# Deformable convolution: a table of pixel pairs, indices in two groups, four gathers issued at once

## Chip, cores and metric

The kernel runs on one core of a Trainium2 chip. The metric is the device time of one execution in microseconds (us); lower is better. Names of engines: PE is TensorE, DVE is VectorE, ACT is ScalarE, POOL is GpSimd, SP is SyncE, which here only issues DMAs.

## What is computed

The network has four residual layers over four images of 56 x 56 pixels with 128 channels, float32: window attention (L0), a selective-scan block (L1), a deformable convolution (L2), window attention again (L3). Each layer gets the group-normalized input and its result is added to the input. The change is in the third layer, whose reference is, cut:

```python
offsets = conv3x3(x, offset_w) + offset_b            # 18 channels: dy, dx for 9 taps
py = row + ky + dy;  px = column + kx + dx
y0, x0 = floor(py), floor(px);  wy, wx = py - y0, px - x0
# gather(y, x): the 128 channels of pixel (y, x), zero outside of the image
val = gather(y0, x0) * (1-wy) * (1-wx) + gather(y0, x0+1) * (1-wy) * wx \
    + gather(y0+1, x0) * wy * (1-wx) + gather(y0+1, x0+1) * wy * wx
out = einsum('bhwkc,kcf->bhwf', val, kernel) + bias
```

So every output pixel reads, for each of nine taps, four neighbouring pixels at a place that the data decides.

## The kernel before

The images are worked on one after the other; `run` calls the four layers for an image b, and all tensors of an image stay in SBUF as [128 channels, 3136 pixels]. Tiles and their waits come from a tile framework: it derives the semaphores from which instruction writes and reads which part of which tile, and also from pools that take over memory of pools closed before. The order on each engine is the order in which the code is written (`manual_schedule`).

**The table.** `deform_prepare` (L1218) makes one table per image in DRAM, 58 x 58 entries (the image with a border of one, TR = 58) of 4 x 128 floats, 2 KB. Entry (y, x) is to hold the four pixels at (y, x), (y, x+1), (y+1, x), (y+1, x+1), so that one index brings all four. At the start it writes zeros to all four tables (L1226, SP); the border keeps them.

**Making the table and the indices.** `deform` (L1230) opens the pool "df" with the index tile `idx` (112 x 252, int32: for each of 28 tiles of 112 pixels, nine taps), and a pool "dc" for the rest of this stage. POOL clears the bordered image `gp` (L1246). Per chunk of 448 pixels DVE normalizes (L1253, `gn_apply`), PE transposes four blocks to pixels by channels (L1257) and ACT copies them to `gt` (L1258). After chunk 3 and after chunk 6 SP writes what is there to the table (L1266): each pixel goes to four places (k = 0 to 3) and the two rows of a 112-pixel tile need a DMA each, so 8 DMAs after chunk 3 and 8 after chunk 6, 56 x 16 or 56 x 12 runs of 512 bytes.

Meanwhile DVE copies the image into `gp` (L1273), PE does the 3 x 3 offset convolution (L1281) in two groups of four and three chunks, ACT adds the bias (L1288), and after both groups PE transposes the offsets (L1293) and DVE adds the base position (L1296). Then DVE works on all 504 columns at once: clip (L1298), cast to integer and back (L1300, L1302), compare and subtract, which makes the floor (L1304, L1305), the index y*58 + x (L1308) plus 59 (L1309), the fractions (L1311, L1312) and the four products of them in `wt` (L1318, eight instructions).

**The gathers.** In a third pool, "dg", which takes over the memory of "dc", `gather(t)` (L1322) issues nine indirect DMAs on POOL for a tile of 112 pixels, one per tap: each brings for 112 indices 2 KB to a row of `g`, which has four buffers. `weigh` (L1330) multiplies the far and the near half of three taps by their weights and adds them (DVE, L1338 to L1340), `turn` (L1342) transposes the two remaining pixels back and adds them up in PSUM (PE L1351, ACT L1352), `product` (L1354) multiplies by the kernel every four tiles (L1358) and `add` (L1361) adds to x. The loop at L1367 calls gather, weigh and turn for t = 0 to 27; the framework lets POOL run ahead as far as the four buffers of `g` go. L3 of the same image follows.

Of the kernel before, what the change touches and what calls it, by code (L numbers as in the profile page):

```python
# [10 lines left out]
F32 = mybir.dt.float32  # L11
F32R = mybir.dt.float32r
I32 = mybir.dt.int32
AF = mybir.ActivationFunctionType
ALU = mybir.AluOpType
# [4 lines left out]
P = 128  # L20
HW = 56
L = HW * HW
CH = 448
NCK = L // CH
# [11 lines left out]
QB = 112  # L36
# [13 lines left out]
KK = 9  # L50
TR = HW + 2
# [27 lines left out]
class _Net:  # L79
# [1138 lines left out]
    def deform_prepare(self):  # L1218


        nc, tc = self.nc, self.tc
        self.tables = [self.dpool.tile([TR * TR, 4 * P], F32, tag=f"tab{b}", name=f"tab{b}") for b in range(self.B)]
        z = self.keep.tile([116, 4 * P], F32, tag="z", name="zero")
        nc.vector.memset(z, 0.0)
        for t in self.tables:
            nc.sync.dma_start(  # L1226
                t.rearrange("(a b) c -> a b c", a=116), z[:, None, :].to_broadcast([116, TR * TR // 116, 4 * P])
            )

    def deform(self, b, x):  # L1230

# [2 lines left out]
        nc, tc, w = self.nc, self.tc, self.w["L2"]  # L1234
        tab = self.tables[b]
        n2 = NTB * KK
        nq = CH // QB
        with tc.tile_pool(name="df", bufs=1) as s1, tc.tile_pool(name="df_ps", bufs=1, space=PSUM) as s1x, tc.manual_schedule():
            idx = s1.tile([QB, n2], I32, tag="idx", name="idx")
            wps = s1x.tile([P, 2, 512], F32, tag="wt", name="wt")  # L1240
            nw = 4 * KK * NTB // 2
            wts = [wps[:QB, i, :nw].rearrange("q (n k) -> q n k", k=4) for i in range(2)]
            with tc.tile_pool(name="dc", bufs=1) as sb, tc.tile_pool(name="dc_ps", bufs=6, space=PSUM) as ps:
                bank = lambda name: ps.tile([P, 512], F32, tag="mm", name=name)
                gp = sb.tile([P, TR, TR], F32, tag="gp", name="gp")
                nc.gpsimd.memset(gp, 0.0)  # L1246
                gn = self.group_norm(sb, ps)
                xg = sb.tile([P, L], F32, tag="xg", name="xgd")
                gt = sb.tile([QB, NTB, P], F32, tag="gt", name="gt")
                tv = tab.rearrange("(t r x) (k c) -> r x t k c", r=2, x=TR, k=4)  # L1250
                for c in range(NCK):
                    cols = slice(c * CH, (c + 1) * CH)
                    self.gn_apply(xg[:, cols], x[:, cols], gn)  # L1253
                    pt = bank("pgt")
                    for i in range(nq):
                        t = c * nq + i
                        nc.tensor.transpose(pt[:QB, i * P : (i + 1) * P], xg[:, t * QB : (t + 1) * QB], self.ident)  # L1257
                    nc.scalar.copy(gt[:, c * nq : (c + 1) * nq, :].rearrange("q t c -> q (t c)"), pt[:QB, :])  # L1258
                    if c in (3, NCK - 1):
                        ts = slice(0 if c == 3 else 4 * nq, (c + 1) * nq)  # L1260
                        for k in range(4):
                            for r in range(2):

                                y = r + 1 - k // 2
                                dst = tv[y % 2, 1 - k % 2 : 1 - k % 2 + HW, y // 2 + ts.start : y // 2 + ts.stop, k, :]
                                nc.sync.dma_start(dst, gt[r * HW : (r + 1) * HW, ts, :])  # L1266
                gv = xg.rearrange("p (h w) -> p h w", w=HW)
                of = sb.tile([P, 2, CH], F32, tag="of", name="of")
                pos = sb.tile([QB, 2 * n2], F32, tag="pos", name="pos")
                for g in range(2):  # L1270
                    n = min(4, NCK - 4 * g)
                    rows = slice(32 * g, min(HW, 32 * g + 32))
                    nc.vector.tensor_copy(gp[:, 1 + rows.start : 1 + rows.stop, 1 : 1 + HW], gv[:, rows, :])  # L1273
                for g in range(2):
                    n = min(4, NCK - 4 * g)
                    pf = bank("pf")
                    for k in range(KK):
                        ky, kx = k // 3, k % 3
                        for j in range(n):
                            c = 4 * g + j  # L1280
                            nc.tensor.matmul(  # L1281
                                pf[32 * j : 32 * j + 32, :CH].rearrange("p (h w) -> p h w", w=HW),
                                lhsT=w["offset_w"][:, k * 32 : (k + 1) * 32],
                                rhs=gp[:, 8 * c + ky : 8 * c + ky + 8, kx : kx + HW],
                                start=(k == 0),
                                stop=(k == KK - 1),
                            )
                    nc.scalar.activation(of[: 32 * n, g, :], pf[: 32 * n, :CH], AF.Identity, bias=w["offset_b"][: 32 * n, :])  # L1288
                for g in range(2):
                    n = min(4, NCK - 4 * g)  # L1290
                    pt = bank("pof")
                    for i in range(nq):
                        nc.tensor.transpose(pt[:QB, i * P : i * P + 32 * n], of[: 32 * n, g, i * QB : (i + 1) * QB], self.ident[: 32 * n, : 32 * n])  # L1293
                    view = lambda t: t[:, 4 * g * nq * 2 * KK : (4 * g + n) * nq * 2 * KK].rearrange("q (j i s) -> q j i s", j=n, s=2 * KK)
                    src = pt[:QB, :].rearrange("q (i j s) -> q j i s", j=4, s=32)[:, :n, :, : 2 * KK]
                    nc.vector.tensor_add(view(pos), src, view(self.w["C"]["base"][:QB, :]))  # L1296

                nc.vector.tensor_scalar(pos, pos, -1.0, float(HW), ALU.max, ALU.min)  # L1298
                fi = sb.tile([QB, 2 * n2], I32, tag="fi", name="fi")
                nc.vector.tensor_copy(fi, pos)  # L1300
                fl = sb.tile([QB, 2 * n2], F32, tag="fl", name="fl")
                nc.vector.tensor_copy(fl, fi)  # L1302
                up = sb.tile([QB, 2 * n2], F32, tag="up", name="up")
                nc.vector.tensor_tensor(up, fl, pos, ALU.is_gt)  # L1304
                nc.vector.tensor_sub(fl, fl, up)  # L1305
                fl2 = fl.rearrange("q (n s) -> q n s", s=2)
                ix = sb.tile([QB, n2], F32, tag="ix", name="ix")
                nc.vector.scalar_tensor_tensor(ix, fl2[:, :, 0], float(TR), fl2[:, :, 1], ALU.mult, ALU.add)  # L1308
                nc.vector.tensor_scalar_add(idx, ix, float(TR + 1))  # L1309
                fr = sb.tile([QB, 2, 2 * n2], F32, tag="fr", name="fr")  # L1310
                nc.vector.tensor_sub(fr[:, 1, :], pos, fl)  # L1311
                nc.vector.tensor_scalar(fr[:, 0, :], fr[:, 1, :], -1.0, 1.0, ALU.mult, ALU.add)  # L1312
                for k in range(4):
                    wy = fr[:, k // 2, :].rearrange("q (n s) -> q n s", s=2)[:, :, 0]
                    wx = fr[:, k % 2, :].rearrange("q (n s) -> q n s", s=2)[:, :, 1]
                    for i in range(2):
                        half = slice(i * n2 // 2, (i + 1) * n2 // 2)
                        nc.vector.tensor_mul(wts[i][:, :, k], wy[:, half], wx[:, half])  # L1318
            with tc.tile_pool(name="dg", bufs=2) as sb, tc.tile_pool(name="dg_ps", bufs=2, space=PSUM) as ps:
                patch, turned, made = {}, {}, {}  # L1320

                def gather(t):  # L1322
                    patch[t] = sb.tile([QB, KK, 4 * P], F32, tag="g", name="g", bufs=4)
                    for k in range(KK):
                        nc.gpsimd.indirect_dma_start(  # L1325
                            out=patch[t][:, k], out_offset=None, in_=tab[:, :],
                            in_offset=bass.IndirectOffsetOnAxis(ap=idx[:, t * KK + k : t * KK + k + 1], axis=0),
                        )

                def weigh(t):  # L1330

# [35 lines left out]
                for t in range(NTB + 2):  # L1367
                    c, i = divmod(t, nq)
                    if t < NTB:
                        gather(t)  # L1370
                        weigh(t)
                    if c >= 1 and i == 1:
                        add(c - 1)
                    if t < NTB:
                        turn(t)
                    if c >= 1 and i == 0:
                        product(c - 1)
# [110 lines left out]
```

## Time and profile before

| | |
|---|---|
| median of 3 runs | 13458.64 us (13451.59 to 13462.05) |
| the profiled execution | 13245.72 us |
| its span | 13243.9 us, 218251 instructions |
| busy PE / DVE / ACT / POOL | 88% / 72% / 57% / 75% |
| gathers (L1325) | 1008, 940.5 us busy on POOL, 933 ns each |
| table writes (L1266) | 64 DMAs, 448 KB (32) and 336 KB (32) |
| zeroing (L1226) | 4 DMAs of 6728 KB |
| DMA moved in all | 344.60 MB |

The profile is of one execution. Its page has the span in 40 slices, in which a digit is the busy share in tenths. A row of a group has the line, the engine, the operation, what is written from what, the count, then busy time or durations; after "idle before" or in brackets stands how long the engine was idle before it, and what ended that. In the chain of waits each row is start, length and what the end waited for at that time; "issue" is time in which the engine waited for nothing that the profile shows, and SPq is SP's DMA queue. In busy times by stretch the columns are the stretch, its length, busy time (and instructions) of PE, PE's weight loads, DVE, ACT and POOL, then PE's granted clock, the DMA share and GB/s.

### The profile page before, as it was taken

The numbers are of one execution on the slowest core, as the hardware profiler recorded it, in microseconds if no ns is written. First come the engines' busy times: TensorE is split into PE (matmuls) and PEld (weight loads), VectorE is DVE, ScalarE is ACT, GpSimd is POOL, SyncE is SP. The second block draws the span as 40 slices with busy tenths as digits, with TensorE's granted clock in tenths as the row PEclk, the third lists the DMA queues.
The fourth block names the chain that finished last, engine by engine and source line by source line (L and its number), as shares of the span: only waits on it lengthen the run. The fifth ranks groups of instructions, "written<-read, shape, count | busy, mean of one in ns | idle before, by whom it ended". The sixth has DMA issues, their size and how long they took to land. (4 is left out here: it accounts for less than half of the span.)

```text
span 13243.9 us, 218251 instructions
## 1 busy us (share of the span) xinstructions
PE 11713.7 (88%) x85716; PEld 7459.5 (56%) x85716; DVE 9575.5 (72%) x11831; ACT 7563.6 (57%) x19130; POOL 9941.6 (75%) x6852
## 2 busy tenths in 40 slices
PE   8999995699898999579989899957999989995799
PEld 4448884444544888444454488834445448883444
DVE  6649996665665999666466499966646649996664
ACT  5567772356556777235655677723565567772356
POOL 4949995488494999548849499954975949995497
PEclk9999997799999999779999999977999999996799
DMA  2000004200000000420000000042000000004200
GB/s 100 1 14 4 5 4 118 78 1 6 6 1 14 4 5 4 120 75 1 8 4 1 14 5 5 4 125 70 1 9 2 1 14 5 5 4 130 65 1 6
DMA packets 181178, 344.60 MB, mean 26 GB/s; under 512 B 20104, under 2 KB 101416, under 8 KB 180024
## 3 DMA queue, kind: packets, MB, share of 16 engines
q0 software_dynamic: 80640, 231.28, 6.3%
q1 hardware_dynamic: 99224, 97.83, 2.4%
q8 instruction: 678, 11.11, 0.4%
q14 instruction: 348, 2.85, 0.1%
q10 hardware_dynamic: 288, 1.53, 0.0%
HBM read 256.04 MB, written 74.52 MB: 25 GB/s over the span
## 5 line engine op out<-in xcount | busy, mean ns | idle before, releaser
L555 POOL TENSOR_TENSOR es<-es,e 128x896 f32<-128x896 f32 x2016 | 4158.8, 2088 | 133.0 <-ACT e L549 75.0
L350 DVE TENSOR_REDUCE mx<-pm 128x1 f32<-128x512 f32 (+1 forms) x4928 | 3056.5, 670 | 1411.1 <-PE pm L349 795.8
L549 ACT ACTIVATE e<-pst 128x448 f32<-128x448 f32 (+1 forms) x5600 | 2677.6, 544 | 1893.3 <-PE pst L547 1348.1
L1066 DVE TENSOR_TENSOR_SCAN hs<-da,dbu 128x928 f32<-128x928 f32 x1792 | 3633.0, 2070 | 53.2 <-ACT dbu L1059 29.3
L1075 POOL TENSOR_TENSOR hs<-hs,cb 128x896 f32<-128x896 f32 x1792 | 3486.9, 1963 | 26.0 <-ACT carry L1070 20.8
L349 PE MATMUL pm<-ks,qs 32*128 32x512 f32 (+1 forms) x9856 | 2911.8, 636 | 13.4 <-DVE nm L371 7.8
L547 PE MATMUL pst<-qs,ks 32*128 32x448 f32 x11200 | 2685.4, 547 | 0.0
L1084 PE MATMUL yt<-w_C,hs 128*116 128x128 f32 x14336 | 1865.8, 273 | 1.1 <-POOL hs L1075 1.1
L542 PE MATMUL pst<-nm,sel 32*128 32x448 f32 x5600 | 1638.7, 614 | 0.0
L1084 PEld LDWEIGHTS yt<-w_C,hs 128*116 128x116 f32 x14336 | 1570.5, 135 | 2.1 <-POOL hs L1075 2.1
L1048 PE MATMUL dbu<-dgb,ut 112*128 112x224 f32 x7168 | 1258.5, 298 | 268.8 <-DVE hs L1066 268.7
L571 PE MATMUL po<-e,va 128*32 128x448 f32 (+1 forms) x11200 | 1352.4, 551 | 0.1
L349 PEld LDWEIGHTS pm<-ks,qs 32*128 32x128 f32 x9856 | 924.3, 186 | 745.2 <-DVE mx L350 618.9
L1325 POOL DMA_INDIRECT g<-tab,idx x1008 | 940.5, 933 | 452.9 <-issue 425.8
L1048 PEld LDWEIGHTS dbu<-dgb,ut 112*128 112x128 f32 x7168 | 945.3, 192 | 534.2 <-DVE hs L1066 524.2
L1002 ACT ACTIVATE da<-dl,A 128x112 f32<-128x112 f32 x3584 | 1194.6, 383 | 0.1
L547 PEld LDWEIGHTS pst<-qs,ks 32*128 32x128 f32 x11200 | 1098.0, 185 | 102.6 <-issue 13.7
L1351 PE MATMUL pvt<-w_C,g 112*128 112x112 f32 x2016 | 404.5, 367 | 729.3 <-issue 607.8
L542 PEld LDWEIGHTS pst<-nm,sel 32*128 32x128 f32 x5600 | 570.6, 184 | 740.2 <-DVE mx L350 387.1
L1352 ACT COPY vt<-pvt 128x336 f32<-128x336 f32 x336 | 147.2, 438 | 1188.0 <-PE pvt L1351 1184.5
L1351 PEld LDWEIGHTS pvt<-w_C,g 112*128 112x128 f32 x2016 | 315.2, 203 | 823.1 <-issue 784.2
L1070 ACT COPY carry<-hs 128x32 f32<-128x32 f32 x1792 | 397.5, 222 | 623.3 <-DVE hs L1066 615.2
(230 smaller groups left out, 15791.4 us busy)
## 6 DMA issues: line engine op xcount, KB each, us to landing
tab<-zero SPq DMA_DIRECT2D x4, 6728.0 KB
g<-tab,idx POOLq DMA_INDIRECT x1008, 3.5
tab<-gt SPq DMA_DIRECT2D x32, 448.0 KB
dl_d<-dl SPq DMA_DIRECT2D x28, 448.0 KB
dl<-dl_d SPq DMA_DIRECT2D x56, 224.0 KB
tab<-gt SPq DMA_DIRECT2D x32, 336.0 KB
out_dram<-x SPq DMA_DIRECT2D x28, 224.0 KB
x<-in_x_dram SPq DMA_DIRECT2D x21, 224.0 KB
```

The lines of the kernel that those rows point to most:

```text
L349: nc.tensor.matmul(pm[:, :m], lhsT=qs[head(h), q.start : q.start + P], rhs=ks[head(h), keys], start=True, stop=True)
L350: nc.vector.tensor_reduce(mx[:, home[i][1], h, kc : kc + 1], pm[:, :m], AX.X, ALU.max)
L542: nc.tensor.matmul(t[:, :CH], lhsT=self.sel[head(h), :], rhs=nm[head(h), part(qc)], start=True, stop=False)
L547: nc.tensor.matmul(t[:, :CH], lhsT=ks[head(h), k * KB : (k + 1) * KB], rhs=qs[head(h), part(qc)], start=False, stop=True)
L549: nc.scalar.activation(e[:nk, j, :], t[:nk, :CH], AF.Exp, scale=SCALE)
L555: nc.gpsimd.tensor_tensor(s, es[g - 1, p][:nk] if k == 1 else s, e[:nk], ALU.add)
L571: nc.tensor.matmul(m["po"][head(h), :CH], lhsT=va[:nk, k, head(h)], rhs=src(h)[:nk], start=(k == 0), stop=(k == NKB - 1))
L1002: nc.scalar.activation(m["da"][:, :, n, 2:], dl(), AF.Exp, scale=A[:, j, n : n + 1])
L1048: nc.tensor.matmul(pu[:, 8 * h : 8 * h + 8, 2 + tb * TB : 2 + (tb + 1) * TB], lhsT=made[g]["ut", 2 * r + tb][:, d, :], rhs=made["r", g // ...
L1066: nc.vector.tensor_tensor_scan(flat(pairs[u // 2][:, d % 2]), flat(made[g]["da"][:, r]), flat(banks.pop(u)), 0.0, ALU.mult, ALU.add)
L1075: nc.gpsimd.tensor_tensor(hs, hs, made["r", g // 2]["cb"][:, :, r * HW : (r + 1) * HW], ALU.mult)
L1084: nc.tensor.matmul(sums[q][:YR, e * P : (e + 1) * P], lhsT=hs[:, n, :], rhs=self.ident, start=(n == 0), stop=(n == NST // 2 - 1), is_trans ...
```

## The change

The table's entry becomes a pair of pixels, (y, x) and (y+1, x), 1 KB; the gather still writes 512 floats per index, so it reads two neighbouring entries, (y, x) and (y, x+1). The table has one more entry at the end, which is set to zero by a DMA of its own. Each pixel is now written to two places, so there are 4 table writes after chunk 3 and 4 after chunk 6. The order of the four pixels in a row of `g` changes, and with it which fraction is used for which (`k % 2` for y and `k // 2` for x).

The offset convolution's groups are worked on to their end one after the other: convolution, bias, transposes, and then all of DVE's steps from the position to the weights on that group's columns (288 and 216). The buffers of `g` move from the pool "dg" to the outer pool "df", and the gathers of the first four tiles are issued on POOL after the first group's index, before its fractions; the loop issues those from tile 4 on. The core of the diff:

```diff
-        self.tables = [self.dpool.tile([TR * TR, 4 * P], F32, tag=f"tab{b}", name=f"tab{b}") for b in range(self.B)]
-        z = self.keep.tile([116, 4 * P], F32, tag="z", name="zero")
+        self.tables = [self.dpool.tile([TR * TR + 1, 2 * P], F32, tag=f"tab{b}", name=f"tab{b}") for b in range(self.B)]
+        z = self.keep.tile([116, 2 * P], F32, tag="z", name="zero")
...
+            nc.sync.dma_start(t[TR * TR :], z[:1])
...
+            patch = {}
+
+            def gather(t):
+                patch[t] = s1.tile([QB, KK, 4 * P], F32, tag="g", name="g", bufs=4)
+                for k in range(KK):
+
+                    nc.gpsimd.indirect_dma_start(
+                        out=patch[t][:, k], out_offset=None, in_=tab[:, :],
+                        in_offset=bass.IndirectOffsetOnAxis(ap=idx[:, t * KK + k : t * KK + k + 1], axis=0),
+                    )
+
...
-                        for k in range(4):
+                        for k in range(2):
                             for r in range(2):
 
-                                y = r + 1 - k // 2
-                                dst = tv[y % 2, 1 - k % 2 : 1 - k % 2 + HW, y // 2 + ts.start : y // 2 + ts.stop, k, :]
+                                y = r + 1 - k
+                                dst = tv[y % 2, 1 : 1 + HW, y // 2 + ts.start : y // 2 + ts.stop, k, :]
                                 nc.sync.dma_start(dst, gt[r * HW : (r + 1) * HW, ts, :])
...
-                for g in range(2):
-                    n = min(4, NCK - 4 * g)
                     pt = bank("pof")
...
+                    ts = slice(4 * g * nq, (4 * g + n) * nq)
+                    ns = slice(ts.start * KK, ts.stop * KK)
+                    both = lambda t: t[:, 2 * ns.start : 2 * ns.stop]
+                    view = lambda t: both(t).rearrange("q (j i s) -> q j i s", j=n, s=2 * KK)
+                    nc.vector.tensor_add(view(pos), src, view(base))
+
+                    nc.vector.tensor_scalar(both(pos), both(pos), -1.0, float(HW), ALU.max, ALU.min)
+                    nc.vector.tensor_copy(both(fi), both(pos))
+                    nc.vector.tensor_copy(both(fl), both(fi))
+                    nc.vector.tensor_tensor(both(up), both(fl), both(pos), ALU.is_gt)
+                    nc.vector.tensor_sub(both(fl), both(fl), both(up))
+                    fl2 = both(fl).rearrange("q (n s) -> q n s", s=2)
+                    nc.vector.scalar_tensor_tensor(ix[:, ns], fl2[:, :, 0], float(TR), fl2[:, :, 1], ALU.mult, ALU.add)
+                    nc.vector.tensor_scalar_add(idx[:, ns], ix[:, ns], float(TR + 1))
+                    if g == 0:
+                        for t in range(4):
+                            gather(t)
+                    nc.vector.tensor_sub(both(fr[:, 1, :]), both(pos), both(fl))
+                    nc.vector.tensor_scalar(both(fr[:, 0, :]), both(fr[:, 1, :]), -1.0, 1.0, ALU.mult, ALU.add)
+                    for k in range(4):
+                        wy = fr[:, k % 2, :].rearrange("q (n s) -> q n s", s=2)[:, :, 0]
+                        wx = fr[:, k // 2, :].rearrange("q (n s) -> q n s", s=2)[:, :, 1]
+                        for i in range(2):
+
+                            at = slice(max(ns.start, i * n2 // 2), min(ns.stop, (i + 1) * n2 // 2))
+                            if at.start < at.stop:
+                                nc.vector.tensor_mul(wts[i][:, at.start - i * n2 // 2 : at.stop - i * n2 // 2, k], wy[:, at], wx[:, at])
...
                     if t < NTB:
-                        gather(t)
+                        if t >= 4:
+                            gather(t)
                         weigh(t)
```

More of the change, by code (lines that the diff above doesn't have):

```diff
@@ L1226, in deform_prepare @@
             nc.sync.dma_start(
-                t.rearrange("(a b) c -> a b c", a=116), z[:, None, :].to_broadcast([116, TR * TR // 116, 4 * P])
+                t[: TR * TR].rearrange("(a b) c -> a b c", a=116), z[:, None, :].to_broadcast([116, TR * TR // 116, 2 * P])
             )
+            nc.sync.dma_start(t[TR * TR :], z[:1])
     def deform(self, b, x):
@@ L1249, in deform @@
                 gt = sb.tile([QB, NTB, P], F32, tag="gt", name="gt")
-                tv = tab.rearrange("(t r x) (k c) -> r x t k c", r=2, x=TR, k=4)
+                tv = tab[: TR * TR].rearrange("(t r x) (k c) -> r x t k c", r=2, x=TR, k=2)
                 for c in range(NCK):
@@ L1268, in deform @@
                 of = sb.tile([P, 2, CH], F32, tag="of", name="of")
-                pos = sb.tile([QB, 2 * n2], F32, tag="pos", name="pos")
+                pos, fl, up = (sb.tile([QB, 2 * n2], F32, tag=n, name=n) for n in ("pos", "fl", "up"))
+                fi = sb.tile([QB, 2 * n2], I32, tag="fi", name="fi")
+                ix = sb.tile([QB, n2], F32, tag="ix", name="ix")
+                fr = sb.tile([QB, 2, 2 * n2], F32, tag="fr", name="fr")
                 for g in range(2):
@@ L1273, in deform @@
                     nc.vector.tensor_copy(gp[:, 1 + rows.start : 1 + rows.stop, 1 : 1 + HW], gv[:, rows, :])
+                base = self.w["C"]["base"][:QB, :]
                 for g in range(2):
@@ L1293, in deform @@
                         nc.tensor.transpose(pt[:QB, i * P : i * P + 32 * n], of[: 32 * n, g, i * QB : (i + 1) * QB], self.ident[: 32 * n, : 32 * n])
-                    view = lambda t: t[:, 4 * g * nq * 2 * KK : (4 * g + n) * nq * 2 * KK].rearrange("q (j i s) -> q j i s", j=n, s=2 * KK)
                     src = pt[:QB, :].rearrange("q (i j s) -> q j i s", j=4, s=32)[:, :n, :, : 2 * KK]
-                    nc.vector.tensor_add(view(pos), src, view(self.w["C"]["base"][:QB, :]))
-                nc.vector.tensor_scalar(pos, pos, -1.0, float(HW), ALU.max, ALU.min)
@@ L1299, in deform @@
[L1299 to L1318, printed above, removed]
@@ L1319, in deform @@
-            with tc.tile_pool(name="dg", bufs=2) as sb, tc.tile_pool(name="dg_ps", bufs=2, space=PSUM) as ps:
[L1320 to L1328, printed above, removed]
+                    ts = slice(4 * g * nq, (4 * g + n) * nq)
@@ L1330, in weigh @@
+            with tc.tile_pool(name="dg", bufs=2) as sb, tc.tile_pool(name="dg_ps", bufs=2, space=PSUM) as ps:
+                turned, made = {}, {}
                 def weigh(t):
```

## Prediction

> **What bounds the kernel now.** I read the page's slices first, then the groups with GpSimd rows, then for the layer that the diff touches the chain of waits, the timeline and the busy times by stretch.
>
> The slices place the deformable layer: the DMA digits are zero except in four places, once per image.
>
> ```profile
> DMA  2000004200000000420000000042000000004200
> ```
>
> The first digit is the zeroing of the tables, the four pairs 42 are the gathers. Inside the last image, the row of the tile g shows how the 252 gathers (28 tiles of 9) run:
>
> ```profile
> L1325 POOL DMA_INDIRECT g<-tab,idx x252: 929/933/1023, 12052.2 to 12362.8; - x126
> L1338 DVE TENSOR_TENSOR pa<-g,wt x84: 943/962/964, 12058.5 to 12366.3; 112x768 f32<-112x768 f32 x84
> ```
>
> From the first start to the last, (12362.8 - 12052.2) / 251 = 1.237 us each: 0.933 busy and 0.30 before the next, without a hole in 311 us. DVE has three products of 0.96, 0.95 and 0.95 us for every three gathers, 2.86 us in 3.71, and waits for gathers. So GpSimd's issue sets the pace, and the end of the layer moves only if that pace or the first gather moves. What ends last before the first gather is in the chain of waits:
>
> ```profile
> 12021.16 0.59 ACT gt L1258
> 12021.81 0.33 SPq L1266
> ...
> 12044.82 1.35 SPq L1266
> 12046.17 0.04 issue
> 12046.22 4.84 DMA tab<-gt
> 12051.47 0.72 issue
> 12052.19 1.02 POOL g L1325
> ```
>
> ACT's fourth copy ends at 12021.75; then come 16 table writes on SP, whose last lands at 12051.06; 1.13 us later the first gather starts. The timeline shows that the indices were ready nearly ten microseconds earlier:
>
> ```profile
> 12037.86 0.46 DVE L1296 TENSOR_TENSOR pos<-pof,w_C 112x288 f32<-112x288 f32 x1 [16.14 <-PE pof L1293]
> ...
> 12042.25 0.29 DVE L1309 TENSOR_SCALAR idx<-ix 112x252 int32<-112x252 f32 x1
> ...
> 12052.19 1.02 POOL L1325 DMA_INDIRECT g<-tab,idx  x1 [36.21 <-issue]
> ```
>
> Thus two things stand before a gather: the table (12051.06) and the indices (12042.5). The busy times from the fourth copy to the first gather, for the four images:
>
> ```profile
> 2109.40:2141.40 32.00, 16.62 (x143) 6.65 (x141) 7.59 (x19) 3.02 (x5) 0.02 (x1) 0.77 0.74 201
> 5416.80:5447.90 31.10, 16.67 (x143) 6.66 (x141) 7.59 (x19) 3.02 (x5) 0.03 (x1) 0.77 0.76 207
> 8719.60:8749.50 29.90, 15.65 (x142) 5.79 (x140) 7.59 (x19) 2.82 (x5) 0.06 (x1) 0.84 0.78 215
> 12021.80:12052.20 30.40, 16.57 (x143) 6.64 (x141) 7.59 (x19) 3.02 (x5) 0.01 (x1) 0.78 0.78 212
> ```
>
> The second column is the length: 123.4 us over four images. The last two are DMA share and GB/s; no compute engine is busy for more than 56% of it.
>
> **What the Trainium skill says.** "DMA: Bandwidth & Descriptors", section "Why a DMA increments its semaphore by 16 and not by 1": a copy spreads over the largest number of engines, up to 16, that divides the slowest dimension on both sides. Here that is 56 rows, so 14 engines. The trace agrees: each image has 12,768 packets on SP's queue, which is 8 x 56 x 16 + 8 x 56 x 12 = 12,544 rows of 512 B plus 16 x 14 for the ends, and the DMA share inside the writes stands at eight or nine tenths, where 14/16 is 0.875. The writes are thus limited by the DMA engines and not by SP's issuing. The same section says that one descriptor moves one contiguous run of the last dimension: a gather of 512 floats at one index stays one run of 2 KB, though a table row is now 1 KB. No run here shows the new form. "SBUF — State Buffer", section "SBUF: two separate sides": GpSimd cannot write descriptors while DVE runs a two-port operation such as an fp32 copy. In the gather stage of the trace DVE has two-tensor products only, and the gathers hold 929 to 933 ns; the change puts some casts beside gathers.
>
> **The change part by part.**
>
> *Table writes, 16 to 8 per image.* Bytes go from 6.42 to 3.21 MB, packets from 12,768 to 6,384. Of the stretch before the first gather I take as not scaling 0.06 us to the issue, about 1.1 us until data flows (an estimate from the GB/s by slices), and 1.13 us from landing to gather: 2.3 us together. The rest halves: (32.0 + 31.1 + 29.9 + 30.4 - 4 x 2.3) / 2 = 57.1 us saved, 14.3 per image. In the last image the first gather then starts at about 12037.9. Bounds: if 3.5 us of the last write's 4.84 us is latency (a lone gather takes 3.5 us from issue to landing), 1.75 us less per image is saved, 50 in all. If SP's issue were the limit, 8 x 1.62 us + 4.84 + 1.13 = 19.0 us instead of 16.2, that is 46. ACT's copies are no limit: the seventh, which the second group of writes needs, ends at 12024.2, while SP is at the first four writes until 12027.
>
> *Indices in two groups.* Were they left at 12042.5, they would end last and cut the gain to 9 us per image. The first group needs PE's first 72 of 126 offset matmuls, whose copy starts on ACT at 12030.56; four transposes (0.65) follow, so DVE begins at about 12032.0. From the rows at 288 and 504 elements: 0.46 (add), 3 x 0.31 (clip and two casts, from 0.42 at 504), 2 x 0.44 (from 0.68), 0.30, 0.23, and eight gaps of 0.04: 3.1 us. Indices at 12035.1, gather possible at 12035.8. The table, at 12037.9, is last by 2 us, so this part ends up hidden; at most it would give 57.1 + 4 x 2 = 65 if the table were faster than I think. PE now waits for ACT between the two groups (about 1.4 us), which delays the second group to 12039.9.
>
> *DVE's extra instructions.* 17 more per image (68 in all), about 0.2 us each beyond what splitting saves. The second group with its weights takes about 0.38 + 3 x 0.27 + 2 x 0.37 + 0.25 + 0.21 + 0.37 + 0.27 + 4 x 0.26 + gaps = 4.5 us and ends at 12044.4. Queued behind it is the first product, whose three gathers land 6.3 us after the first gather's start (12052.19 to 12058.5 before), at 12044.2. That is a tie. If DVE is late by a few us, nothing is lost: four tiles of g are 36 gathers, 44.5 us ahead, and DVE makes up 0.85 us per three gathers. Cost zero. The casts and scalings of the second group run beside gathers; should they lock GpSimd out, that is five of them of 0.3 us, 1.5 us per image, 6 us in all. I take zero and keep 6.
>
> *g in the outer pool, four gathers ahead.* The 36 gathers stand on GpSimd directly after the clearing of gp, as before; only the place of the buffers differs, so that they no longer wait for what lay in the same memory. The built program has the first gather waiting for the eight table writes and DVE alone, and the second group's index write waits for no gather. Zero by itself, but without it the gathers would wait for the second group (12043).
>
> *Zeroing.* 27.6 MB become 13.8, with four row writes more on SP. It runs from 3 us to some 310 us under the first layer, which uses no DMA; SP's next write comes later. Zero.
>
> *Gathers.* The same 1,008 of 224 KB. Lower and upper price of the new form: same row, 1.237 us; I take that. Better is excluded, as issue and not bytes sets it (DMA share 0.66 in the stage).
>
> Sum: -57. The profiled execution took 13245.7 us (span 13243.9), which makes 13188.6. The median of the runs shown is 13458.64, 213 us more for the same program; the saved stretch is DMA time on which no matmul bears, so I take the same 57 off: 13401.5.
>
> **Rivals.**
>
> *The writes don't get faster by half.* Rows of 512 B now go to addresses 1 KB apart instead of 2 KB. If the write rate falls from 229 GB/s (6.42 MB in about 28 us) to near half, the table is late as before. For: nothing here shows that address pattern. Against: the same run length on the same 14 engines. With the rate down by a third, 21 us of writing instead of 14, the saving is 7 us per image, 28: 13431; with it halved, 13457, no change. Middle: 13444.
>
> *The gathers get slower, and the time ends above before.* 1,008 gathers are the only part that multiplies. If two rows at one index cost GpSimd more descriptor work, the price is 1,008 x the added time; 0.057 us each (6% of 0.933) eats the 57 us, 0.083 is slower by 0.2%. A full doubling of 0.933 would be +940 us. Against: the built program lists one run of 112x512 per gather, as before, with only the multiplier of the index halved. At 10%: 94 - 57, 13496.
>
> *The indices or DVE are last.* If a hidden order keeps gathers behind the second group (12043.2), 9 us per image, 36: 13423. The built order speaks against it.
>
> **How the numbers follow.** Forecast, 0.74 (own range 13389 to 13413: 46 to 65 saved, and some 5 us of spread of the runs shown). Indices last, 0.06, also faster. Writes slower, 0.12, half of it still faster by over 0.2%. Gathers slower, 0.07, of which 0.05 beyond 0.2%. The last 0.01 is other. About 0.2%, 27 us, is what a measurement of this kernel can tell from no change. Faster 0.85, same 0.09, slower 0.06. The range from 13380 to 13446 takes in the forecast, late indices and half the slower writes.
>
> **What would show it.** Right: 6,384 packets per image in the table writes, the first gather 16 to 17 us after ACT's fourth copy instead of 30 to 32, gathers still 1.237 us apart, and the chain of waits still going through the table's last write. Wrong: a gather row above 933 ns, a table stretch above 20 us, or DVE's second group named before the first gather.

## Result, and the profile after

The median is 13414.49 us (13404.82 to 13430.00, 7 runs) against 13458.64 us before (13443.35 to 13476.57, 7 runs): 44 us less, ratio 0.9964 with a 95% interval of 0.9954 to 0.9973, which is 36 to 62 us. The prediction was 13401.5 us, 57 less; its forecast by itself had the range 13389 to 13413, so the result lies just past it.

In the profile of before that the prediction was made from (13245.7 us) the gather stage takes 327 us per image; in the profile of after (13430.0 us, the longest of its seven runs) it takes 385, and the experiments show that the kernel before has the long stage too where its time is near 13455. So the two profiles are not to be compared in that stage. The stretch before the first gather can be compared: in the kernel before it is 30.9 us beside the short stage and 30.6 beside the long one.

The page of the changed kernel has the table's bytes halved. Its two largest queues are the gathers' (q0) and SP's (q1), of which the latter had 99,224 packets and 97.83 MB before; after packets and MB stands the share of the 16 DMA engines' span:

```profile
q0 software_dynamic: 80640, 231.28, 6.0%
q1 hardware_dynamic: 73696, 71.21, 1.7%
```

Of the 26.6 MB that are gone, four times 3.21 MB were table writes and 13.8 MB zeros. The gathers have the 80,640 packets and 231.28 MB that they had before, which fits one run of 2 KB per index, as forecast. The table writes of one image are 6,384 packets. The chain of waits before the first gather of the last image, in the profile of after:

```profile
12162.84 0.59 ACT gt L1271
12163.43 0.02 SPq L1279
...
12172.67 1.25 SPq L1279
12173.92 0.04 issue
12173.96 6.03 DMA tab<-gt
...
12180.05 0.72 issue
12180.78 1.02 POOL g L1248
```

It is the same chain as before, ACT's copy, SP's issues, the last write, the gather, but 17.4 us long where it was 30.4. The busy times from the fourth copy to the first gather, by image (second column the length, last two DMA share and GB/s):

```profile
2110.92:2128.57 17.65, 16.26 (x140) 6.24 (x138) 5.46 (x18) 2.97 (x6) 0.00 (x0) 0.96 0.68 183
5470.86:5488.05 17.19, 15.69 (x141) 5.73 (x139) 5.46 (x18) 2.89 (x6) 0.00 (x0) 0.99 0.69 188
8818.22:8834.57 16.35, 15.59 (x137) 6.22 (x138) 5.46 (x18) 2.40 (x5) 0.00 (x0) 0.96 0.72 197
12163.42:12180.78 17.36, 16.14 (x140) 6.17 (x138) 5.47 (x18) 2.81 (x6) 0.00 (x1) 0.96 0.69 186
```

They sum to 68.6 us, against 123.4 before: 55 us gone from these stretches. What is different further on is the gather stage. The instructions of g and those that use it:

```profile
L1248 POOL DMA_INDIRECT g<-tab,idx x1008: 927/934/1142, 2128.6 to 12532.5; - x168
L1349 DVE TENSOR_TENSOR pa<-g,wt x336: 943/961/964, 2134.8 to 12554.0; 112x768 f32<-112x768 f32 x168
```

The durations are those of before, but the last image now has its first gather at 12180.8 and its last at 12532.5, 352 us where the profile of before has 311. GpSimd is not slower: it stands still eight to ten times per image, almost always at the first gather of a new tile, for 1.3 to 8.9 us. The timeline at one such place, cut:

```profile
12231.46 0.44 ACT L1363 COPY vt<-pvt 128x336 f32<-128x336 f32 x1 [16.36 <-issue]
12231.95 1.38 PE L1362 MATMUL pvt<-w_C,g 112*128 112x112 f32 x6 [15.42 <-issue]
12244.06 1.12 ACT L1363 COPY vt<-pvt 128x336 f32<-128x336 f32 x3 [12.16 <-remote]
12244.30 0.94 POOL L1248 DMA_INDIRECT g<-tab,idx  x1 [7.68 <-remote]
12244.55 6.90 PE L1362 MATMUL pvt<-w_C,g 112*128 112x112 f32 x42 [11.22 <-ACT vt L1363]
```

ACT copies the results of three groups of six transposes one right after the other from 12244.06 on; the first of these groups had been started on PE at 12208.7. It looks as if PE's transposes are reported done late, ACT waits for that (this profile lacks part of the semaphore records of the stage, hence "remote" and "issue" as releasers), PE waits for ACT to free its buffers, and GpSimd for a buffer of g. Whether the change makes this or only meets it was the first thing to settle.

### The profile page after: what moved, and what is told of

It reads as the page before. It is cut to its first block, busy times and chain, and to the rows that moved or that the text cites. A ratio compares the mean times of both kernels' runs of the same rounds, so it can differ in the third digit from the quotient of the medians.

```text
span 13428.2 us, 218271 instructions
## 1 busy us (share of the span) xinstructions
PE 11694.2 (87%) x85716; PEld 7452.0 (55%) x85716; DVE 9598.0 (71%) x11883; ACT 7561.2 (56%) x19130; POOL 9947.0 (74%) x6852
## 3 DMA queue, kind: packets, MB, share of 16 engines
q0 software_dynamic: 80640, 231.28, 6.0%
## 5 line engine op out<-in xcount | busy, mean ns | idle before, releaser
L1066 DVE TENSOR_TENSOR_SCAN hs<-da,dbu 128x928 f32<-128x928 f32 x1792 | 3632.7, 2070 | 53.5 <-ACT dbu L1059 30.9
L349 PE MATMUL pm<-ks,qs 32*128 32x512 f32 (+1 forms) x9856 | 2909.3, 634 | 13.4 <-DVE nm L371 7.8
L1363 ACT COPY vt<-pvt 128x336 f32<-128x336 f32 x336 | 141.3, 441 | 1364.8 <-remote 695.0
```

The source lines that it names most:

```text
L349: nc.tensor.matmul(pm[:, :m], lhsT=qs[head(h), q.start : q.start + P], rhs=ks[head(h), keys], start=True, stop=True)
L1066: nc.vector.tensor_tensor_scan(flat(pairs[u // 2][:, d % 2]), flat(made[g]["da"][:, r]), flat(banks.pop(u)), 0.0, ALU.mult, ALU.add)
```

## Experiments

Four sets, each on one chip with the kernel before beside it: the first four rows of the table, the next four, then two and two. "First gather" is the time from the end of ACT's fourth copy to the start of the first gather, a mean over the four images of the profiled execution; "stage" is from the first gather to the end of the last kernel product of the layer. Kernels with one run have only that time, and are read from their traces.

| kernel | median us, runs | before beside it | ratio (95%) | first gather | stage per image |
|---|---|---|---|---|---|
| before again | 13241.1 (1) | 13239.2 | | 30.9 | 327 |
| pairs only | 13203.9 (13) | 13239.2 | 0.9977 (0.9969 to 0.9985) | 25.2 | 327 |
| early only | 13244.3 (21) | 13239.2 | 1.0001 (0.9995 to 1.0008) | 30.7 | 327 |
| changed kernel again | 13182.7 (5) | 13239.2 | 0.9956 (0.9942 to 0.9970) | 17.2 | 327 |
| half of the writes | 13173.0 (5) | 13239.5 | 0.9946 (0.9932 to 0.9959) | 13.3 | 327 |
| half gathers | 13184.1 (1) | 13239.5 | | 17.1 | 326 |
| pairs, g in the outer pool | 13193.6 (6) | 13239.5 | 0.9968 (0.9956 to 0.9980) | 20.3 | 327 |
| writes in three portions | 13173.3 (5) | 13239.5 | 0.9950 (0.9936 to 0.9964) | 15.2 | 327 |
| far product in SBUF | 13232.6 (1) | 13243.2 | | 17.0 | 333 |
| before, a third time | 13240.0 (1) | 13243.2 | | 30.7 | 327 |
| writes in four portions | 13397.7 (5) | 13455.0 | 0.9956 (0.9942 to 0.9970) | 14.9 | 383 |
| before, last | 13458.4 (1) | 13455.0 | | 30.6 | 383 |

**Is the long stage the change's?** No edit, the kernel before.

> The kernel before, unchanged, profiled once more. Its profiled execution of 13245.7 us lies 213 us below the runs shown (13458.64). In that profile the gather stage of each image ran 310.7 us from first to last gather and 16 us on to the end of the layer; in the profile of the changed kernel it ran 352 us and 28 to 35 us, with the waits at PE's transposes. Theory A: those waits are in the timed runs of both kernels, and the profile of before is the exception. Then this execution is near 13458 us and shows a gather stage of about 350 + 30 us per image. Theory B: the waits come from the change. Then the gather stage is 311 + 16 us here, and if the time is near 13458 the 213 us are in the other layers.

This chip (13239 us in 33 runs of before) doesn't have the long stage: 13241.1 us, stage 327 us. It could not decide between A and B, nor could the third profile of before, on another chip with the short stage:

> The kernel before once more, for its profile on whatever chip this is. If its time is near 13458, theory A of the first run says that its gather stage is about 380 us per image instead of 327 and nothing else has changed; theory B of the first run says that the 219 us are in the other layers. If it is near 13239 this says nothing new.

The last set fell on a chip where before takes 13455:

> The kernel before, profiled beside the last kernel. If this chip's time is near 13458 instead of 13239, its gather stage tells how much of the late transposes it has (theory A of the first run: about 382 us per image instead of 327); if it is near 13239, it only bounds the spread of the undisturbed stage: 327 us within 1 us.

The kernel before has a stage of 382.8, 383.5, 382.5 and 381.4 us there, and its other layers are as elsewhere. ACT's copies of the transposes, L1352, and what their idle time ended on, in this kernel:

```profile
L1352 ACT COPY vt<-pvt x336: 438/438/459, 2148.0 to 12593.0; 128x336 f32<-128x336 f32 x168
  remote: 703.7, 57
  PE pvt L1351: 359.1, 154
  issue: 329.9, 58
```

The same row of the changed kernel in the profile of the result, L1363:

```profile
  remote: 695.0, 65
  PE pvt L1362: 343.0, 143
  issue: 323.5, 60
```

and of the changed kernel in the first set, on the chip with 13239:

```profile
  PE pvt L1362: 1123.7, 307
```

The two columns are us and times. The first two sum to 1393 and 1361 us, the third to 1124. So the first half of theory A holds: the late transposes come with the place of the run, for both kernels alike, and not with the change. The profile of before is no exception, though; three of the four sets are like it. By its times the result is from the chip of the last set or from one like it, and whether it is the chip or something else at that time is not shown: each set was on its chip once.

**Which part carries the gain.** Pairs only: the table, its zeroing, its writes and the order of the weights as in the change; indices in one group, g in the pool "dg" and gathers from the loop as before.

```diff
-                        for k in range(4):
+                        for k in range(2):
```

> The table of pairs alone: indices in one group, gathers from the loop, g in the pool that takes over the memory of dc. Table theory: the writes end 16 to 17 us after ACT's fourth copy, but the indices end at 20.8, so the first gather starts at about 21.5 instead of 30.9: 9 us per image, ratio 0.9973 (13421 us). Rival, that starting the gathers early is what carries the gain: ratio 1.000. Rival, that the pairs themselves lengthen the gather stage: ratio above 0.999.

35 us less by the medians, close to the 36 of the table theory, but that is luck: the first gather comes at 25.2 us, not 21.5, and four times 5.7 us are only 23, which the interval (20 to 41 us) also holds. The chain of waits of this kernel's last image says why it is late:

```profile
12025.09 0.31 DVE wt L1319
...
12025.60 0.72 issue
12026.33 1.02 POOL g L1326
```

It no longer waits for the table but for DVE's last weight, which ends 3.7 us after the last index (L1310 of this kernel, 12021.7): g lies where DVE's fractions lay. The next kernel is this one with g moved from "dg" to "df":

```diff
-                    patch[t] = sb.tile([QB, KK, 4 * P], F32, tag="g", name="g", bufs=4)
+                patch[t] = s1.tile([QB, KK, 4 * P], F32, tag="g", name="g", bufs=4)
```

> Table of pairs and g in the outer pool, but indices in one group and all gathers issued from the loop. With the table of pairs alone the first gather came 25.3 us after ACT's fourth copy though the indices were there at 20.7. Theory, that it waited for DVE's weights because g took over memory that DVE still read: now it starts 0.7 us after the indices, at 21.5, and the ratio to before is about 0.9971 (against 0.9977 with pairs alone and 0.9957 with the index groups as well). Rival, that the place of g does nothing: 25.3 us, 0.9977.

20.3 us, 0.3 us after the end of the index row, which itself came at 20.0 and so sooner than the forecast took: the place of g is worth 5 us per image once the table is out of the way. Early only, the change with the table of four pixels, its 16 writes and the old order of the weights:

```diff
-                        for k in range(2):
+                        for k in range(4):
```

> The changed kernel with the table of four pixels and its 16 writes: indices in two groups, four gathers ahead, g in the outer pool. Table theory: the gathers wait for the table, first gather 30 to 32 us after ACT's fourth copy as before, ratio 1.000 (0.999 to 1.001). Rival, that starting early carries the gain: ratio about 0.997.

No gain, with a narrow interval. Groups, place and early issue gain only behind a faster table: 30.9 us (before), 25.2 (pairs), 20.3 (and place of g), 17.2 (and index groups). The changed kernel itself, beside these:

> The changed kernel as it is, on the chip of the other runs: ratio 0.9964 as before (0.9954 to 0.9973), first gather 16 to 17.7 us after ACT's fourth copy. Theory A of the first run: gather stage about 350 + 30 us per image, as in the first profile of it; should this execution run without the waits, it is near 13245 - 55 = 13190 us.

56.5 us less than before on this chip, where the forecast was 57. An agreement this close is luck, as the interval is 40 to 77 us; the traces of this set have 55.

**What ends last now.** Half of the writes (the kernel leaves out the lower pixel of each pair, so its result is not the network's):

```diff
-                        for k in range(2):
+                        for k in range(1):
```

> The changed kernel, which leaves out half of its table writes: the lower pixel of each pair stays zero (4 writes per image instead of 8). It asks what ends last once the table is out of the way. Theory: the writes would end about 10 us after ACT's fourth copy, so the first group's indices (13.2 us) decide and the first gather starts at 13.9 us instead of 17.2: 3.3 us per image less than the changed kernel, 13 us in all, ratio to before about 0.9947. Rival, that something else holds the first gather (the clearing of gp, the buffers, SP): it stays at 17 us, ratio 0.9957.

13.3 us: the first group's indices, whose row ends at 13.0, are the next limit, 3.9 us below the table. Writes in three portions, which begin sooner:

```diff
-                    if c in (3, NCK - 1):
-                        ts = slice(0 if c == 3 else 4 * nq, (c + 1) * nq)
+                    if c in (1, 3, NCK - 1):
+                        ts = slice({1: 0, 3: 2, NCK - 1: 4}[c] * nq, (c + 1) * nq)
```

> The changed kernel with its table writes in three portions, after chunks 1, 3 and 6, instead of two: 12 writes of the same 3.21 MB that begin 1.7 us sooner. Theory, that the DMA engines limit the writes: the last lands 1.7 us sooner, first gather at about 15.5 us, 7 us less in all, ratio about 0.9951. Rival, that SP's issue of each write counts: four more writes of 1.6 us make the last later, first gather at 17 us or more, ratio 0.9957 or above.

15.2 us with 12 writes instead of 8, so the bytes set the end and not the number of writes. The medians put it 9 us under the changed kernel, but on different chips and within both intervals; the 2 us per image are shown by the traces alone. Four portions:

```diff
+                    if c in (0, 1, 3, NCK - 1):
+                        ts = slice({0: 0, 1: 1, 3: 2, NCK - 1: 4}[c] * nq, (c + 1) * nq)
```

> The changed kernel with its table writes in four portions, after chunks 0, 1, 3 and 6: 16 writes of the same 3.21 MB that begin 2.6 us sooner than in the changed kernel. Three portions gave a first gather at 15.2 us and a ratio of 0.9950. Theory, that bytes limit: 14.3 to 14.5 us, 3 us less than three portions over four images, ratio about 0.9948. Rival, that the fixed part of each write now counts: 15.2 us or later, ratio 0.995 or above.

14.4, 15.6, 14.4 and 15.3 us: two images at what bytes alone would give, two at the value of three portions. Neither theory fits all four, and there is no clear gain over three; the ratio of 0.9956 belongs to a chip with the long stage and can't be set beside the 0.9950.

**What sets the gathers' pace.** Half gathers (the right pair is left out and the left one weighed in its place, so again the result is not the network's; the edit of the gather alone is shown):

```diff
-                        out=patch[t][:, k], out_offset=None, in_=tab[:, :],
+                        out=patch[t][:, k, : 2 * P], out_offset=None, in_=tab[:, :],
```

> The changed kernel with gathers of 256 instead of 512 floats per index (the right pair is left out, and the left one is weighed in its place): the same 1008 gathers of 112 rows with half the bytes. Theory, that GpSimd's issue per gather is the pace: still 1.237 us apart, 933 ns busy, stage 310.7 us, time as the changed kernel's on this chip. Rival, that the bytes or the DMA engines are the pace: shorter spacing, the stage toward 250 us.

The row of g in this kernel:

```profile
L1248 POOL DMA_INDIRECT g<-tab,idx x1008: 929/933/1127, 2117.2 to 12301.9; - x168
```

933 ns with half the bytes, and from first to last gather 310.7 us: the pace is GpSimd's issue and not the bytes. Whether it goes by the gather or by its 112 rows is open, as no run had other rows. Far product in SBUF:

```diff
-                        pa = ps.tile([P, 2, 512], F32, tag="pa", name="pa", bufs=1)
+                        pa = sb.tile([P, 2, 512], F32, tag="pa", name="pa", bufs=1)
```

> The changed kernel with DVE's far product kept in SBUF instead of PSUM. In the first profile of the changed kernel PE's transposes ended up to 34 us late in the gather stage while DVE was busy, and each image lost some 58 us there; on two other chips nothing of it was seen. Theory A, that PE's writes to PSUM stand behind DVE's traffic there: where this execution shows the late transposes at all, they are much shorter (gather stage and end under 345 us instead of 385). Theory B, that it is something of that chip or execution which has nothing to do with PSUM: late as before where the kernel before run beside it is near 13458, and none where it is near 13239. Where none are seen: stage of 311 + 16 us, time as the changed kernel's, unless two inputs from SBUF on DVE hold up GpSimd's descriptors, which would lift the gathers above 933 ns.

It didn't meet the long stage, so it says nothing on PSUM there. It shows another thing:

```profile
L1248 POOL DMA_INDIRECT g<-tab,idx x1008: 930/937/1674, 2127.6 to 12352.4; - x168
```

Single gathers now take up to 1.67 us, and from first to last gather it is 317.4 us instead of 310.8. Two things are new: DVE's first product (L1349) writes to SBUF, and its sum (L1351) takes both inputs from there. The timeline of this kernel says which of them it is:

```profile
2143.87 0.96 DVE L1351 TENSOR_TENSOR g<-g,pa 112x768 f32<-112x768 f32 x1
2144.19 1.44 POOL L1248 DMA_INDIRECT g<-tab,idx  x1 [0.30 <-issue]
...
2147.09 0.96 DVE L1351 TENSOR_TENSOR g<-g,pa 112x768 f32<-112x768 f32 x1
2147.17 1.67 POOL L1248 DMA_INDIRECT g<-tab,idx  x1 [0.30 <-issue]
```

The first of these gathers starts when the sum has 0.64 us left and takes 0.51 us more than 0.93; the second, with 0.88 us left, takes 0.74 more. So it goes through the whole trace: 98 of the 105 gathers over 1.0 us start while a sum runs, and their extra time is what the sum has left less some 0.13 us; the other seven are the first gather of each image and three beside the second group's index and weight steps. Of the 620 gathers that start during one of the two products none takes more than 0.94 us, and neither does any of the 321 that start during a sum in the changed kernel of the first set, where one input is in PSUM. It is the sum with both inputs in SBUF.

## Why the prediction was right, and where its size was off

**Table writes (57.1 us).** Right in mechanism. In the first set the first gather moved from 30.92 to 17.17 us: 13.8 per image, 55 in all. The mis-sized term is what doesn't scale: 2.3 us were taken; two lengths with half the bytes between them give 2 x 17.17 - 30.92 = 3.4 us. The packets in these traces show where it lies: the first starts 0.9 us after the copy in both, but from the first to the end of the last it takes 28.5 us before and 15.1 after, 0.8 more than half. In the profile of after the last write needed 6.03 us to land, against 4.84 in that of before. The bound of 50, with more latency in the last write, lay on the right side.

**Indices hidden by the table.** Right: the first group was put at 13.4 us after ACT's fourth copy and ended at 12.6 to 13.2 in the profile of after; the table is last by some 4 us, where 2 were expected.

**DVE's extra instructions and casts beside gathers at nothing.** Right: the first product started 5.9 to 6.6 us after the first gather, as before (6.2 to 6.4). The first three gathers of the last image took 1.02, 1.03 and 1.14 us, together 0.3 us more than before, and those of the other images 0.1 or less, against a bound of 1.5. The count of 17 more instructions per image was too high: the pages have 11,883 against 11,831, which is 13.

**g's place "zero by itself, but without it the gathers would wait for the second group (12043)".** Undersized where it was tried: without it the gathers wait for the weights too, which with indices in one group is 25.2 us against 20.3. No run has two groups with g in its old place.

**Gathers unchanged.** Right: 933 to 934 ns, with half the bytes too. None of the rivals came in: the writes did take about half the time, the gathers did not get slower, the indices are not last.

**Why 44 and not 57.** The sum said that the same 57 us come off the median because no matmul bears on the saved stretch. The stretch behaves so: of the two profiles with the long stage, the one of before (before, last) has 122.5 us in it and the one of after 68.6, 54 us less. But the sum also took the stage behind it as equal. Over four images it is 1530.2 us in that profile of before and 1538.4 in that of after, 8.2 us given back, so that stretch and stage together fall by some 46. That may be the price of one execution: the profile of after is the longest of its seven runs, 15.5 us over their median, and the kernel with four portions, whose writes alone differ, has 1530.6 us there. Single images lie between 380.9 and 385.7 us. With the result's interval of 36 to 62 us, 57 is not excluded either; what is shown is the 54 to 55 us of the stretch, and why the median has 44 is open. Not predicted at all was what the 213 us between the profile of before and the median were: they were named and put aside, and they sit in the very stage that the argument followed. The forecast asked only whether the saved stretch carries over, not whether the change touches this stage; that the stage is about as long with both kernels was luck.

**Open.** Why PE's transposes are reported late on one chip. In the profile of after the copies of finished groups start up to 40 us after PE's last transpose, while the first six groups of the last image start within some 0.1 us of DVE's results. That points to the way from PE to ACT, PE's report or ACT's notice of it, and not to DVE or GpSimd, but no experiment on that chip took anything of it away. Two causes can be struck out by comparing the two profiles of before: PE's granted clock in the stage is 0.59 to 0.60 with the long stage and 0.60 with the short one, and a gather's DMA packet takes 0.166 us on average against 0.165. One thing does differ: of the semaphore records the long profile has 1122 to 1199 per image in this stage, the short one 4387, and outside of it hardly one is missing. Whether that is a mark of the cause, or the recording itself holds PE up there, no run tells.

## What to carry to other kernels

A transfer that ends last before a stage is worth its bytes: find the part of its time that scales, by two lengths if there are two. What hides behind it comes out one by one: here the place of a buffer and the order of index making were worth nothing beside the slow table and 8 us per image together once the table was short. When a profile and the runs shown differ by more than the effect that is forecast, find the stage of the difference first: it may be the one that the change moves.

## What the runs showed of the hardware that was not expected

On one chip of at least four the same program takes 13455 instead of 13239 us, all of it in the gather stage, 55 us per image, at the same granted clock. The seven runs before in the result (13443 to 13477) match that chip's nine (13444 to 13472); that it is the chip, and not its state at that time, is not shown.

An indirect DMA of 112 rows costs GpSimd 0.933 us and 0.30 us before the next, with rows of 1 KB as of 2 KB.

A DVE sum with both inputs in SBUF holds up a gather's issue that starts while it runs, by what is left of the sum less 0.13 us: single gathers went from 0.93 to 1.67 us, and first to last gather took 6.6 us longer. A gather that had started before the sum was not stretched. "SBUF — State Buffer", section "SBUF: two separate sides", of the Trainium skill names two SBUF inputs as a holder of the shared ports only against a GpSimd instruction that reads SBUF; the measurement fits this, and what the section says of the one that starts first, for an issue that takes its indices from SBUF. That it is the indices which wait is argued, not shown.

The table writes go in rows of 512 B, and halving the rows' distance in DRAM from 2 KB to 1 KB did not slow the single one: a packet takes 30 ns on average in both kernels. From the first packet to the end of the last it is 225 GB/s before and 213 after (first set); the difference is the 0.8 us above that did not halve.
